# One layer of convolution and attention: the first image begins with the middle taps, its weights are built in small steps, weight loads move to ScalarE's queue, scaled output sums are put off

## The chip, the cores and the metric

The kernel runs on one core of one Trainium2 chip. Its time is the device time of one execution in microseconds (us). All arithmetic is float32. The engines are named TensorE (PE in profiles; its weight loads are PEld), VectorE (DVE), ScalarE (ACT), GpSimd (POOL) and SyncE (SP, which here only issues DMAs).

## The reference

Four images x of 128 channels and 64 by 64 pixels go through two layers. The change touches only the first. After a group norm it sums three padded convolutions (7x7, 5x5 and 3x3, 128 to 128 channels) with a non-local attention block and its residual, applies a relu and adds x:

```
g = _gn(x)                                  # 32 groups of 4 channels
y = conv2d(g, w7, b7, 3) + conv2d(g, w5, b5, 2) + conv2d(g, w3, b3, 1)
f = einsum('bcn,bcm->bnm', theta, phi) / sqrt(64)     # 4096 x 4096 scores for each image
out = einsum('bcm,bnm->bcn', g_x, softmax(f))         # then a 1x1 convolution, plus g
x = x + relu(y + nonlocal(g))               # what the kernel computes of layer 0
```

The second layer takes the pixels as 4096 tokens: a layer norm, a state-space block in both directions, another layer norm, a batch norm over all tokens, and a recurrence over the tokens. Its code is the same before and after.

## The kernel before

**Stages.** `conv_attention` does layer 0 for all images (it fills the first 1736 us of the profiled span), `mamba` and `recurrence` do layer 1. The running image values live in one SBUF tensor `t` of four images; the outputs of layer 0 overwrite the image they belong to.

**Convolution.** The three kernels are summed into one 7x7 kernel. Its middle row stays as it is (`wc`). The other rows are applied as a polynomial product: the input rows are combined into forms and multiplied by combined weights at the points 0, +U, -U, +V, -V and infinity. This gives eight pieces of work, numbered `m`: 0 and 5 (the two end points, which also take the middle row on other rows), 1 and 2 (plus and minus U), 3 and 4 (plus and minus V), 6 and 7 (the middle row alone, with the input rows as they are). A piece with m below 6 has three products n = 0, 1, 2, each with a weight tile of its own: 18 tiles of 576 KB, `wd`, in HBM. `convolve` loads them one by one into `wt` (L377, a pool of two buffers, on SyncE's queue), multiplies (L364), and combines the results `eo` on ScalarE (L383), VectorE (L385 to L391) and GpSimd (L397 to L419). Pieces 1 and 3 only keep their result (`mid`). Piece 2 adds and subtracts it and writes four output phases: one on GpSimd, and three scaled ones on ScalarE, put off with `later`. Piece 4 adds to these four: one on GpSimd (L411) and three scaled ones at once on VectorE, in two halves each (L414).

**Attention.** A step handles 512 queries: eight iterations of `scores` (L437, then the exponential on ScalarE, L439, into `ex`, four buffers) and `values` (L448), while VectorE sums the exponentials into `es` (L452, L454). Then comes one piece of convolution, with `divide` (the reciprocal, L460) and `collect` (L468 to L470, which adds finished attention outputs to `t`) between its products. So an image is eight steps, and layer 0 is 32 steps. I number them 0 to 31. `forms` builds the inputs of the step's convolution on ScalarE and GpSimd while the attention runs.

**Order of pieces.** `ORDER = (1, 2, 0, 6, 7, 5, 3, 4)` for images 0 to 2, and `LAST = (1, 2, 3, 4, 6, 7, 5, 0)` for image 3.

**Order on the engines.** TensorE and ScalarE are under `manual_schedule`: their instructions stand as the program writes them. VectorE, GpSimd and SyncE are ordered by the scheduler when the program is built, and every engine then takes its own list strictly in order. `later(f)` appends to the list `late`, from which each iteration of the attention takes one entry: it decides where the call stands in the program.

**Weights.** The generator `weights` loads w7, w5 and w3 into the space of image 1 in `t`, sums them (L512, L513), forms sums and differences along x (`thirds`, L520 to L522, over seven rows at once), copies the middle row to `wc` (L526), and then forms the 18 tiles (`pair`, L540 to L542, and `store`, L531, L533). Everything up to and including pieces 1 and 2 is asked for before step 0, the ends before step 1, pieces 3 and 4 before step 2. Image 1 is loaded over this space afterwards (L1641); `statistics` (L238) reads it.

**Finish.** `finish(b)` queues eight parts for the image before: a load of x into `xr` (L475, SyncE, two buffers), a relu on ScalarE (L477), an add on GpSimd (L478).

Of the kernel before, what the change touches and what calls it, by code (L numbers as in the profile page):

```python
# [10 lines left out]
F32 = mybir.dt.float32  # L11
AF = mybir.ActivationFunctionType
ALU = mybir.AluOpType
# [3 lines left out]
P = 128  # L17
NC = 512
# [135 lines left out]
def conv_attention(nc, tc, k, a, t, B, H, W, flags, load, mem, loads):  # L154
# [21 lines left out]
    KB, PC = H // 4, W // 2  # L176
# [10 lines left out]
    with ExitStack() as ctx:  # L187
# [176 lines left out]
                    nc.tensor.matmul(pm[:, e, :], wt, src, start=(i == 0), stop=(i == len(terms) - 1))  # L364
            return pm

        def convolve(b, m, f):

            image = t[:, b * T : (b + 1) * T].rearrange("p (k g j c x) -> p g j x k c", g=2, j=4, c=PC, x=2)
            base = None  # L370
            for n in range(3):
                if f[n] is None:
                    continue
                wt = wc
                if m < 6:
                    wt = fm.tile([P, 9, P], F32, tag="wt", name="wt")
                    nc.sync.dma_start(wt, wd[3 * m + n])  # L377
                fn = [v + (u,) for v, u in zip(f[n], (wt, wc))]
# [3 lines left out]
                by = BY.get(m, 1.0)  # L382
                nc.scalar.mul(eo[:, 1, :], pm[:, 1, :], by / 2)  # L383
                for e, op in enumerate((ALU.add, ALU.subtract)):
                    nc.vector.scalar_tensor_tensor(eo[:, e, :], pm[:, 0, :], by / 2, eo[:, 1, :], ALU.mult, op)  # L385
# [12 lines left out]
                out = lambda j: image[:, n - 1, j]  # L398
                in_ = lambda v: v.rearrange("p x (k c) -> p x k c", c=PC)
                if keep:  # L400
                    mid[n] = eo
                elif m == 2:
                    nc.gpsimd.tensor_tensor(out(0), in_(mid[n]), in_(eo), ALU.add)
                    nc.gpsimd.tensor_tensor(mid[n], mid[n], eo, ALU.subtract)
                    for j, v, by in ((2, out(0), UU), (1, in_(mid[n]), U), (3, in_(mid[n]), U * UU)):
                        later(nc.scalar.mul, out(j), v, by)
                elif m == 4:
                    u = wk.tile([P, 2, KB // 2 * PC], F32, tag="u", name="u", bufs=2)
                    nc.gpsimd.tensor_tensor(u, mid[n], eo, ALU.add)
                    nc.gpsimd.tensor_tensor(mid[n], mid[n], eo, ALU.subtract)  # L410
                    nc.gpsimd.tensor_tensor(out(0), out(0), in_(u), ALU.add)  # L411
                    for j, v, by in ((2, u, VV), (1, mid[n], V), (3, mid[n], V * VV)):
                        for x in range(2):
                            nc.vector.scalar_tensor_tensor(  # L414
                                out(j)[:, x], in_(v)[:, x], by, out(j)[:, x], ALU.mult, ALU.add
                            )
                else:
                    j = {0: 0, 5: 3, 6: 1, 7: 2}[m]
                    nc.gpsimd.tensor_tensor(out(j), out(j), in_(eo), ALU.add)  # L419
                yield  # L420

        def queries(n):
# [33 lines left out]
        def divide(n, acc, es):  # L456
            den = ps_c.tile([P, NC], F32, tag="c", name="den")
            nc.tensor.matmul(den, k.ones, es[:, 0, :], start=True, stop=True)
            att = wk.tile([P, NC], F32, tag="att", name="att", bufs=3)
# [23 lines left out]
        def later(f, *args):  # L483

            late.append(lambda: f(*args))
# [17 lines left out]
        def weights():  # L503

            w = t[:, T : T + 63 * P].rearrange("p (y x o) -> p y x o", y=7, x=9)
            free = t[:, T + 63 * P : T + 90 * P].rearrange("p (n o) -> p n o", o=P)
            w5 = free[:, 0:25].rearrange("p (y x) o -> p y x o", y=5)
            w3 = wc.rearrange("p (y x) o -> p y x o", y=3)
            nc.sync.dma_start(w[:, :, 0:7, :], a["w7t"].rearrange("i (y x) o -> i y x o", y=7))
            nc.sync.dma_start(w5, a["w5t"].rearrange("i (y x) o -> i y x o", y=5))  # L510
            nc.sync.dma_start(w3, a["w3t"].rearrange("i (y x) o -> i y x o", y=3))
            nc.vector.tensor_tensor(w[:, 1:6, 1:6, :], w[:, 1:6, 1:6, :], w5, ALU.add)  # L512
            nc.gpsimd.tensor_tensor(w[:, 2:5, 2:5, :], w[:, 2:5, 2:5, :], w3, ALU.add)  # L513

            nc.vector.scalar_tensor_tensor(w[:, 3, 3, :], k.ident, 2.0, w[:, 3, 3, :], ALU.mult, ALU.add)

            def thirds(g, new):

                ac = free[:, 0 : new.shape[1], :]
                nc.vector.tensor_tensor(ac, g[0], g[2], ALU.add)  # L520
                nc.gpsimd.tensor_tensor(new, ac, g[1], ALU.subtract)
                nc.vector.tensor_tensor(g[1], ac, g[1], ALU.add)  # L522
# [12 lines left out]
            def pair(m, at):  # L535

                spare = [fm.tile([P, 9, P], F32, tag="wt", name="ws") for _ in range(2)]
                made = []
                for g, e, f in zip(lots, (slot[0], slot[2]), (slot[1], spare[0])):
                    nc.vector.scalar_tensor_tensor(e, g[:, 2], at * at, g[:, 0], ALU.mult, ALU.add)  # L540
                    nc.vector.scalar_tensor_tensor(f, g[:, 1], at, e, ALU.mult, ALU.add)
                    nc.vector.scalar_tensor_tensor(e, g[:, 1], -at, e, ALU.mult, ALU.add)  # L542
                    made.append((f, e))
                store(m, slot[3], *(v[0] for v in made))
                store(m + 1, spare[1], *(v[1] for v in made))

            pair(1, U)
            yield
            for m, i in ((0, 0), (5, 2)):
                store(m, slot[i], *(g[:, i] for g in lots))  # L550
            yield
            pair(3, V)
            yield

        phi = big.tile([P, NT // 2, P], F32, name="phi")
        gT = big.tile([P, NT, IC], F32, name="gT")
        gn, mid, atts, xl, late = {}, {}, {}, [], []
# [20 lines left out]
        for n in range(N):  # L578
            b, q = divmod(n, NQ)
            more = b + 1 < B and q == NQ - 1  # L580
            if n in (1, 2):
                next(making)
            if 3 <= n < B + 2:
                load(n - 2)
            m = (ORDER if b + 1 < B else LAST)[q]
            f = []
            making_forms = forms(m, f)
            next(making_forms, None)
            if b + 1 < B and q == NQ - 3:
# [15 lines left out]
            for i, _ in enumerate(convolve(b, m, f)):  # L605
# [1093 lines left out]
```

## Time and profile before

| | |
|---|---|
| three runs | 3225.29, 3225.89 and 3230.95 us, median 3225.89 |
| the profiled execution | 3225.68 us, span 3224.0 us |
| layer 0 in the span | 0 to 1736 us (the attention steps from 35.57 us) |
| TensorE matmul, busy | 2959.4 us (92%) |
| VectorE, ScalarE, GpSimd, busy | 2279.3, 1805.0 and 1805.3 us |
| bytes by DMA | 224.15 MB, mean 70 GB/s |

The shares are averages over stages that differ. The chain of waits on the page, followed back from the last instruction, reaches 1765 us and no further, so it tells nothing of layer 0, where the change lies. There the boundaries of the 32 steps are read from TensorE's timeline: a step begins at the first score matmul after a convolution. A step's length is then compared with that of a step of the same piece without a stall.

### The profile page before, as it was taken

Reading aid. Unit: us, or ns where it says so; the run is one execution under the profiler, and the core shown is the slowest. Engines: PE = TensorE matmul, PEld = TensorE weight load, DVE = VectorE, ACT = ScalarE, POOL = GpSimd, SP = SyncE. Lnnn points to the kernel's source line nnn. Section 1 sums busy time; section 2 is a strip of 40 time slices with the busy share of each in tenths; the row PEclk is TensorE's granted clock in tenths of the full one; section 3 lists DMA queues with packets and bytes.
Section 4 is the critical chain, followed back from the end, with each engine's and each line's share of the span. In section 5 each row is a group of like instructions: output and inputs, shape, how many; then the busy total and the mean of one; then the engine's idle time right before and its main releaser. Section 6 shows DMA issues by size and latency. Waiting matters only on the chain. (4 is left out here: it accounts for less than half of the span.)

```text
span 3224.0 us, 42883 instructions
## 1 busy us (share of the span) xinstructions
PE 2959.4 (92%) x15511; PEld 1467.2 (46%) x15511; DVE 2279.3 (71%) x3458; ACT 1805.0 (56%) x3078; POOL 1805.3 (56%) x1369
## 2 busy tenths in 40 slices
PE   5889999899988999899998899999999999999986
PEld 1444444445443544344354354444444444454545
DVE  6676677766876677767666676767667767777667
ACT  3224434333435334343432787887788778888756
POOL 5461757825758446677165266556655664565654
PEclk8999999999999999999998899999999999999988
DMA  4230001100011001021002334333433343334332
GB/s 170 81 138 8 23 31 37 56 15 23 23 38 55 23 8 37 22 64 37 8 23 86 87 93 118 96 93 93 114 91 97 88 113 92 102 93 99 90 113 106
DMA packets 108394, 224.15 MB, mean 70 GB/s; under 512 B 25679, under 2 KB 29391, under 8 KB 106765
## 3 DMA queue, kind: packets, MB, share of 16 engines
q1 hardware_dynamic: 106956, 220.01, 23.7%
q8 instruction: 125, 2.05, 0.3%
q10 hardware_dynamic: 1216, 1.31, 0.1%
q14 instruction: 97, 0.79, 0.1%
HBM read 200.83 MB, written 20.44 MB: 69 GB/s over the span
## 5 line engine op out<-in xcount | busy, mean ns | idle before, releaser
L454 DVE TENSOR_TENSOR es<-es,ex 128x1024 f32<-128x1024 f32 x448 | 722.5, 1613 | 117.9 <-ACT ex L439 79.5
L439 ACT ACTIVATE ex<-pf 128x1024 f32<-128x1024 f32 x512 | 500.8, 1023 | 490.6 <-PE pf L437 381.4
L437 PE MATMUL pf<-theta,phi 64*128 64x512 f32 x2048 | 523.2, 629 | 58.2 <-ACT ex L439 56.8
L448 PE MATMUL acc<-ex,gT 128*64 128x512 f32 x2048 | 495.1, 609 | 13.5 <-ACT ex L439 13.5
L1147 POOL TENSOR_TENSOR ct<-ct,Cst 128x512 f32<-128x512 f32 x128 | 169.3, 1323 | 404.8 <-DMA ct<-csmem 363.5
L437 PEld LDWEIGHTS pf<-theta,phi 64*128 64x128 f32 x2048 | 175.0, 189 | 382.7 <-ACT ex L439 242.6
L364 PE MATMUL pm<-yf,wt 128*128 128x256 f32 x1152 | 293.6, 388 | 23.1 <-DMA wt<-wd 23.1
L1113 ACT ACTIVATE lt<-lt,cs 128x128 f32<-128x128 f32 x1024 | 312.1, 390 | 0.0
L383 ACT ACTIVATE eo<-pm 128x256 f32<-128x256 f32 x88 | 33.8, 384 | 481.7 <-PE pm L364 481.7
L448 PEld LDWEIGHTS acc<-ex,gT 128*64 128x64 f32 x2048 | 127.9, 137 | 356.6 <-issue 330.2
L364 PEld LDWEIGHTS pm<-yf,wt 128*128 128x128 f32 x1152 | 218.1, 193 | 98.7 <-issue 54.5
L335 POOL TENSOR_TENSOR yf<-yd 128x272 f32<-128x272 f32 x192 | 243.5, 1300 | 0.0
L1048 PE MATMUL pb<-tl,wbc_fwd 128*64 128x512 f32 x512 | 236.8, 606 | 2.4 <-DVE xT L1080 2.4
L1048 PE MATMUL pb<-tl,wbc_bwd 128*64 128x512 f32 x512 | 237.4, 606 | 0.0
L397 POOL TENSOR_TENSOR eo<-eo 128x512 f32<-128x512 f32 x48 | 62.9, 1310 | 288.3 <-DVE eo L391 220.3
L419 POOL TENSOR_TENSOR t<-t,eo 128x512 f32<-128x512 f32 x32 | 44.0, 1375 | 301.2 <-DVE eo L389 300.0
L1212 POOL TENSOR_TENSOR yT<-yT,zT 128x512 f32<-128x512 f32 x127 | 167.3, 1327 | 34.7 <-DVE yT L1199 30.5
L1146 DVE TENSOR_TENSOR lt<-lt,gm 128x1024 f32<-128x1024 f32 x128 | 182.5, 1425 | 1.9
L385 DVE SCALAR_TENSOR_TENSOR eo<-pm,eo 128x256 f32<-128x256 f32 x176 | 73.5, 418 | 117.4 <-ACT eo L383 115.0
L1080 DVE SCALAR_TENSOR_TENSOR xT<-px,taps_bwd,xT 128x512 f32<-128x512 f32 x192 | 143.7, 749 | 8.2 <-ACT xT L1074 3.3
L335 POOL TENSOR_TENSOR yf<-yx 128x272 f32<-128x272 f32 x96 | 148.0, 1570 | 1.9
L1179 PE MATMUL y<-lt,xdt 128*64 128x128 f32 x2048 | 141.7, 281 | 7.7 <-PE ptr L1122 3.4
(295 smaller groups left out, 5777.2 us busy)
## 6 DMA issues: line engine op xcount, KB each, us to landing
lt<-csmem SPq DMA_DIRECT2D x128, 512.0 KB, 5.7
wt<-wd SPq DMA_DIRECT2D x72, 576.0 KB, 3.7
ct<-csmem SPq DMA_DIRECT2D x256, 128.0 KB, 5.3
rs<-m SPq DMA_DIRECT2D x31, 512.0 KB, 4.1
t<-in_x SPq DMA_DIRECT2D x4, 2048.0 KB
rows<-after SPq DMA_DIRECT2D x32, 256.0 KB, 4.4
out<-t SPq DMA_DIRECT2D x4, 2048.0 KB, 14.4
wd<-t SPq DMA_DIRECT2D x14, 576.0 KB, 3.3
```

Source lines behind the costliest of these rows:

```text
L335: nc.gpsimd.tensor_tensor(f[:, kx], at(x), at(y), op)
L364: nc.tensor.matmul(pm[:, e, :], wt, src, start=(i == 0), stop=(i == len(terms) - 1))
L437: nc.tensor.matmul(pf[:, e, :], phi[HALF[e], m, :], th[HALF[e]], start=True, stop=True)
L439: nc.scalar.activation(ex, pf, AF.Exp, scale=scale)
L448: nc.tensor.matmul(acc[HALF[e]], gT[:, 2 * m + e, :], ex[:, e, :], start=(m == 0), stop=(m == NT // 2 - 1))
L454: nc.vector.tensor_tensor(es, es, ex, ALU.add)
L1048: nc.tensor.matmul(out, w[i]["bc"][:, tap, bass.ts(c, DS)], src, start=(tap == 0), stop=(tap == KC - 1),)
L1080: nc.vector.scalar_tensor_tensor(at(n), px, taps[:, PAD - n : KC - n], at(n), ALU.mult, ALU.add)
L1113: nc.scalar.activation(v, v, AF.Relu, scale=-1.0, bias=m["b"]["cs"][:, d, m["i"], h : h + 1])
L1146: nc.vector.tensor_tensor(lt, lt, gm.unsqueeze(2).to_broadcast([P, ND, NHEAD, P]), ALU.mult)
L1147: nc.gpsimd.tensor_tensor(m["ct"], m["ct"], Cs[:, cols].unsqueeze(1).to_broadcast([P, NHEAD, P]), ALU.mult)
L1212: eng.tensor_tensor(v, v, gr["z"][d][:, :, half(d, j // 2)], ALU.mult)
```

## The change

1. Image 0 takes its pieces in the order `FIRST = (6, 7, 1, 2, 0, 5, 3, 4)`. Since outputs may now first be written by any piece, `put` keeps a set `begun` and copies (or scales) the first time and adds afterwards. In image 0, attention outputs are collected in the fifth step instead of the third (`att` gets four buffers instead of three).
2. `weights` builds the middle row first and the rest in 24 small pieces, one taken in each iteration of the attention.
3. The loads of weight tiles go to ScalarE's queue: tiles 0 and 1 in the next to last iteration of the attention, tile 2 behind the scaling of the second product.
4. Piece 4 puts off its three scaled sums with `later`, as piece 2 does. Where an output phase has begun, a scaled sum is two VectorE instructions.

```diff
+        def fetch(m, n):
+            wt = fm.tile([P, 9, P], F32, tag="wt", name="wt")
+            nc.scalar.dma_start(wt, wd[3 * m + n])
+            return wt
+            def put(n, j, v, by=1.0):
+                out = image[:, n - 1, j]
+                if (b, n, j) not in begun:
+                    begun.add((b, n, j))
+                    if by == 1.0:
+                        nc.gpsimd.tensor_copy(out, v)
+                    else:
+                        nc.scalar.mul(out, v, by)
+                elif by == 1.0:
+                    nc.gpsimd.tensor_tensor(out, out, v, ALU.add)
+                else:
+                    for x in range(2):
+                        nc.vector.scalar_tensor_tensor(out[:, x], v[:, x], by, out[:, x], ALU.mult, ALU.add)
...
-                    nc.sync.dma_start(wt, wd[3 * m + n])
...
                 nc.scalar.mul(eo[:, 1, :], pm[:, 1, :], by / 2)
+                if wts and n == 1:
+                    wts.append(fetch(m, 2))
...
-                    for j, v, by in ((2, out(0), UU), (1, in_(mid[n]), U), (3, in_(mid[n]), U * UU)):
-                        later(nc.scalar.mul, out(j), v, by)
+                    for j, v, c in ((2, out, UU), (1, in_(mid[n]), U), (3, in_(mid[n]), U * UU)):
+                        later(put, n, j, v, c)
...
-                    for j, v, by in ((2, u, VV), (1, mid[n], V), (3, mid[n], V * VV)):
-                        for x in range(2):
-                            nc.vector.scalar_tensor_tensor(
-                                out(j)[:, x], in_(v)[:, x], by, out(j)[:, x], ALU.mult, ALU.add
-                            )
+                    put(n, 0, in_(u))
+                    for j, v, c in ((2, u, VV), (1, mid[n], V), (3, mid[n], V * VV)):
+                        later(put, n, j, in_(v), c)
...
-            nc.vector.tensor_tensor(w[:, 1:6, 1:6, :], w[:, 1:6, 1:6, :], w5, ALU.add)
-            nc.gpsimd.tensor_tensor(w[:, 2:5, 2:5, :], w[:, 2:5, 2:5, :], w3, ALU.add)
+            sums(3, 4)
             nc.vector.scalar_tensor_tensor(w[:, 3, 3, :], k.ident, 2.0, w[:, 3, 3, :], ALU.mult, ALU.add)
             for s in SLOT:
-                thirds([w[:, :, s[i], :] for i in (0, 1, 3)], w[:, :, s[2], :])
+                thirds(3, 4, s)
+            sums(1, 3)
+            yield
+            sums(4, 6)
             nc.gpsimd.tensor_copy(wc, w[:, 3])
+            yield
+            for s in SLOT:
+                for y in (0, 4):
+                    thirds(y, y + 3, s)
+                    yield
...
+            yield from pair(1, U, (slot[0:2], slot[2:4]), spare)
             for m, i in ((0, 0), (5, 2)):
                 store(m, slot[i], *(g[:, i] for g in lots))
+                yield
+            yield from pair(3, V, [(g[:, 2], g[:, 0]) for g in lots], (slot[1], slot[3]))
...
+        FIRST = (6, 7, 1, 2, 0, 5, 3, 4)
...
-            if n in (1, 2):
-                next(making)
...
                 next(making_forms, None)
+                next(making, None)
+                if m < 6 and i == NB - 2:
+                    wts = [fetch(m, 0), fetch(m, 1)]
                 if late:
                     late.pop(0)()
...
-                    if q != 1:
+                    if q not in ((1, 2, 3) if b == 0 else (1,)):
                         for o in sorted(atts):
                             collect(o, atts.pop(o))
```

`sums(y0, y1)` adds w5 (VectorE) and w3 (GpSimd) to the rows y0 to y1 of w7. `pair` yields after each instruction and after each stored piece.

More of the change, by code (lines that the diff above doesn't have):

```diff
@@ L365, in products, with convolve @@
             return pm
-        def convolve(b, m, f):
-            image = t[:, b * T : (b + 1) * T].rearrange("p (k g j c x) -> p g j x k c", g=2, j=4, c=PC, x=2)
+        def fetch(m, n):
+            wt = fm.tile([P, 9, P], F32, tag="wt", name="wt")
+            nc.scalar.dma_start(wt, wd[3 * m + n])
+            return wt
+        def convolve(b, m, f, wts):
+            image = t[:, b * T : (b + 1) * T].rearrange("p (k g j c x) -> p g j x k c", g=2, j=4, c=PC, x=2)
+            in_ = lambda v: v.rearrange("p x (k c) -> p x k c", c=PC)
+            def put(n, j, v, by=1.0):
[11 more added lines that the diff above has]
+                        nc.vector.scalar_tensor_tensor(out[:, x], v[:, x], by, out[:, x], ALU.mult, ALU.add)
+            by = BY.get(m, 1.0)
             base = None
@@ L373, in convolve @@
                     continue
[L374 to L378, printed above, removed]
+                fn = [v + (u,) for v, u in zip(f[n], (wts[n], wc) if wts else (wc,))]
                 pm = products(fn, (1, 2))
@@ L381, in convolve @@
                 eo = wk.tile([P, 2, KB // 2 * PC], F32, tag=f"mid{n}" if keep else "eo", name="eo", bufs=1 if keep else 4)
-                by = BY.get(m, 1.0)
                 nc.scalar.mul(eo[:, 1, :], pm[:, 1, :], by / 2)
+                if wts and n == 1:
+                    wts.append(fetch(m, 2))
                 for e, op in enumerate((ALU.add, ALU.subtract)):
@@ L397, in convolve @@
                     nc.gpsimd.tensor_tensor(eo, eo, base, ALU.add)
-                out = lambda j: image[:, n - 1, j]
-                in_ = lambda v: v.rearrange("p x (k c) -> p x k c", c=PC)
                 if keep:
@@ L402, in convolve @@
                 elif m == 2:
-                    nc.gpsimd.tensor_tensor(out(0), in_(mid[n]), in_(eo), ALU.add)
+                    begun.add((b, n, 0))
+                    out = image[:, n - 1, 0]
+                    nc.gpsimd.tensor_tensor(out, in_(mid[n]), in_(eo), ALU.add)
                     nc.gpsimd.tensor_tensor(mid[n], mid[n], eo, ALU.subtract)
-                    for j, v, by in ((2, out(0), UU), (1, in_(mid[n]), U), (3, in_(mid[n]), U * UU)):
-                        later(nc.scalar.mul, out(j), v, by)
+                    for j, v, c in ((2, out, UU), (1, in_(mid[n]), U), (3, in_(mid[n]), U * UU)):
+                        later(put, n, j, v, c)
                 elif m == 4:
@@ L410, in convolve @@
                     nc.gpsimd.tensor_tensor(mid[n], mid[n], eo, ALU.subtract)
-                    nc.gpsimd.tensor_tensor(out(0), out(0), in_(u), ALU.add)
-                    for j, v, by in ((2, u, VV), (1, mid[n], V), (3, mid[n], V * VV)):
-                        for x in range(2):
-                            nc.vector.scalar_tensor_tensor(
-                                out(j)[:, x], in_(v)[:, x], by, out(j)[:, x], ALU.mult, ALU.add
-                            )
-                else:
-                    j = {0: 0, 5: 3, 6: 1, 7: 2}[m]
-                    nc.gpsimd.tensor_tensor(out(j), out(j), in_(eo), ALU.add)
+                    put(n, 0, in_(u))
+                    for j, v, c in ((2, u, VV), (1, mid[n], V), (3, mid[n], V * VV)):
+                        later(put, n, j, in_(v), c)
+                else:
+                    put(n, {0: 0, 5: 3, 6: 1, 7: 2}[m], in_(eo))
                 yield
@@ L458, in divide @@
             nc.tensor.matmul(den, k.ones, es[:, 0, :], start=True, stop=True)
-            att = wk.tile([P, NC], F32, tag="att", name="att", bufs=3)
+            att = wk.tile([P, NC], F32, tag="att", name="att", bufs=4)
             nc.vector.reciprocal(att, den)
@@ L511, in weights, with sums, thirds @@
             nc.sync.dma_start(w3, a["w3t"].rearrange("i (y x) o -> i y x o", y=3))
-            nc.vector.tensor_tensor(w[:, 1:6, 1:6, :], w[:, 1:6, 1:6, :], w5, ALU.add)
-            nc.gpsimd.tensor_tensor(w[:, 2:5, 2:5, :], w[:, 2:5, 2:5, :], w3, ALU.add)
-            nc.vector.scalar_tensor_tensor(w[:, 3, 3, :], k.ident, 2.0, w[:, 3, 3, :], ALU.mult, ALU.add)
[L517 to L522, printed above, removed]
+            def sums(y0, y1):
+                nc.vector.tensor_tensor(
+                    w[:, y0:y1, 1:6, :], w[:, y0:y1, 1:6, :], w5[:, y0 - 1 : y1 - 1], ALU.add
+                )
+                z0, z1 = max(y0, 2), min(y1, 5)
+                nc.gpsimd.tensor_tensor(
+                    w[:, z0:z1, 2:5, :], w[:, z0:z1, 2:5, :], w3[:, z0 - 2 : z1 - 2], ALU.add
+                )
+            def thirds(y0, y1, s):
+                v, new = [w[:, y0:y1, s[i], :] for i in (0, 1, 3)], w[:, y0:y1, s[2], :]
+                ac = free[:, 25 : 25 + y1 - y0, :] if y1 - y0 == 1 else free[:, 0 : y1 - y0, :]
+                nc.vector.tensor_tensor(ac, v[0], v[2], ALU.add)
+                nc.gpsimd.tensor_tensor(new, ac, v[1], ALU.subtract)
+                nc.vector.tensor_tensor(v[1], ac, v[1], ALU.add)
+            sums(3, 4)
+            nc.vector.scalar_tensor_tensor(w[:, 3, 3, :], k.ident, 2.0, w[:, 3, 3, :], ALU.mult, ALU.add)
             for s in SLOT:
-                thirds([w[:, :, s[i], :] for i in (0, 1, 3)], w[:, :, s[2], :])
+                thirds(3, 4, s)
+            sums(1, 3)
+            yield
+            sums(4, 6)
             nc.gpsimd.tensor_copy(wc, w[:, 3])
+            yield
[3 more added lines that the diff above has]
+                    yield
             slot = [free[:, bass.ts(i, 9), :] for i in range(3)] + [w[:, 3]]
@@ L533, in store, with pair @@
                     nc.sync.dma_start(wd[3 * m + n], v)
[L535 to L539, printed above, removed]
+            def pair(m, at, places, boths):
+                for g, (e, f) in zip(lots, places):
                     nc.vector.scalar_tensor_tensor(e, g[:, 2], at * at, g[:, 0], ALU.mult, ALU.add)
+                    yield
                     nc.vector.scalar_tensor_tensor(f, g[:, 1], at, e, ALU.mult, ALU.add)
+                    yield
                     nc.vector.scalar_tensor_tensor(e, g[:, 1], -at, e, ALU.mult, ALU.add)
[L543 to L548, printed above, removed]
+                    yield
+                for i in range(2):
+                    store(m + i, boths[i], *(v[1 - i] for v in places))
+                    yield
+            spare = [fm.tile([P, 9, P], F32, tag="wt", name="ws") for _ in range(2)]
+            yield from pair(1, U, (slot[0:2], slot[2:4]), spare)
             for m, i in ((0, 0), (5, 2)):
                 store(m, slot[i], *(g[:, i] for g in lots))
-            yield
-            pair(3, V)
-            yield
+                yield
+            yield from pair(3, V, [(g[:, 2], g[:, 0]) for g in lots], (slot[1], slot[3]))
         phi = big.tile([P, NT // 2, P], F32, name="phi")
         gT = big.tile([P, NT, IC], F32, name="gT")
-        gn, mid, atts, xl, late = {}, {}, {}, [], []
+        gn, mid, atts, xl, late, begun = {}, {}, {}, [], [], set()
         NB = NT // 4
         N = B * NQ
+        FIRST = (6, 7, 1, 2, 0, 5, 3, 4)
         ORDER = (1, 2, 0, 6, 7, 5, 3, 4)
@@ L580, in conv_attention @@
             more = b + 1 < B and q == NQ - 1
-            if n in (1, 2):
-                next(making)
             if 3 <= n < B + 2:
                 load(n - 2)
-            m = (ORDER if b + 1 < B else LAST)[q]
-            f = []
+            m = (FIRST if b == 0 else ORDER if b + 1 < B else LAST)[q]
+            f, wts = [], None
             making_forms = forms(m, f)
@@ L603, in conv_attention @@
             nc.vector.tensor_tensor(es[:, 0, :], es[:, 0, :], es[:, 1, :], ALU.add)
-            for i, _ in enumerate(convolve(b, m, f)):
+            for i, _ in enumerate(convolve(b, m, f, wts)):
                 if i == 0:
-                    if q != 1:
+                    if q not in ((1, 2, 3) if b == 0 else (1,)):
                         for o in sorted(atts):
```

## The prediction

> **What bounds the kernel now.** The chain of waits begins at 1765 us, so for layer 0 I read TensorE's timeline, cut it into the 32 steps, and asked for busy time and clock in single steps. The columns are the stretch, its length, busy time (and count) of PE, PEld, DVE, ACT and POOL, then clock, DMA share and GB/s.
>
> ```profile
> 35.57:119.52 83.95, 51.22 (x192) 21.84 (x192) 59.16 (x44) 21.77 (x25) 46.18 (x25) 0.82 0.37 134
> 119.52:165.12 45.60, 45.33 (x193) 21.39 (x192) 37.25 (x30) 18.32 (x21) 29.63 (x18) 1.00 0.11 39
> 165.12:241.92 76.80, 61.61 (x238) 30.62 (x237) 54.07 (x60) 23.16 (x28) 49.80 (x44) 0.91 0.36 137
> 489.92:545.06 55.14, 49.28 (x196) 22.37 (x195) 44.98 (x39) 20.60 (x23) 36.05 (x22) 0.94 0.10 33
> 545.06:602.38 57.32, 48.40 (x197) 23.50 (x196) 37.37 (x38) 23.20 (x29) 42.45 (x28) 0.91 0.21 68
> ```
>
> Step 1 (second row) is a step without stall: TensorE is busy for 45.33 of 45.60 us at clock 1.00. Undisturbed, TensorE bounds layer 0, and a step with a piece of 1 to 4 lasts 45.6 us. Steps 0, 2, 8 and 9 (the other rows) are far longer, and their clock is below 1. The difference is what can be won. Steps 16 and 24 repeat step 8 (56.08 and 54.13 us), 17 and 25 repeat step 9 (57.06 and 53.01 us), and step 28, after the last image's piece 4, lasts 51.02 against 42.17 us. The waits of TensorE in layer 0 (total, times, longest) name two causes:
>
> ```profile
> PE pf L437 <- ACT ex L439: 56.8, 40, 17.3
> PE pm L364 <- DMA wt<-wd: 23.1, 3, 9.5
> PE den L458 <- DVE eo L385: 10.6, 4, 7.5
> ```
>
> The timeline shows what stands behind them.
>
> ```profile
> 64.52 16.88 DVE L454 TENSOR_TENSOR es<-es,ex 128x1024 f32<-128x1024 f32 x8
> 66.90 2.08 PE L437 MATMUL pf<-theta,phi 64*128 64x512 f32 x4 [17.26 <-ACT ex L439]
> ...
> 187.78 0.69 DVE L238 BATCH_NORM_STATS2 st<-t 128x6 f32<-128x512 f32 x1 [6.20 <-DMA t<-in_x]
> ...
> 496.17 7.11 DVE L414 SCALAR_TENSOR_TENSOR t<-eo,t 128x256 f32<-128x256 f32 x4
> 505.59 3.78 PE L437 MATMUL pf<-theta,phi 64*128 64x512 f32 x8 [5.51 <-ACT ex L439]
> ...
> 576.60 14.32 SPq L475 DMA_DIRECT2D xr<-in_x  x8
> 590.97 68.06 SPq L377 DMA_DIRECT2D wt<-wd  x6
> 595.44 5.22 PE L364 MATMUL pm<-yf,wt 128*128 128x256 f32 x12 [8.65 <-DMA wt<-wd]
> ```
>
> At 66.90 TensorE has waited 17.26 us: an exponential needs a buffer that the sums es free, and these waited until 64.52 behind weight making. In step 2 the statistics stand in VectorE's list between the sums and wait for an image. In step 8 the scaled sums of piece 4 (four in 7.11 us, beside GpSimd) hold up the sums. In step 9 SyncE must first issue the finish loads xr, each waiting for a buffer, and the weight tile comes late.
>
> **Weight loads, won.** Without stall steps 9, 17 and 25 would last 45.60 plus 0.45 us (four transposes) = 46.05. They lose 11.27 + 11.01 + 6.96 = 29.2 us, the slow clock after the wait included. From ScalarE's queue, tiles 0 and 1 are asked for well ahead, and no load of xr is in front. All of the 29.2 goes.
>
> The Trainium skill ("DMA: Bandwidth & Descriptors", section "Issuing engines are not separate DMA queues") says that issuing from several engines saves only the sequencer's issue time. A weight load's issue takes 0.32 us in this trace; an estimate by that rule alone would be three such issues, 1 us instead of 29.2. The trace disagrees here: the tile was not slow but not asked for, the issuing engine waiting in order at 576.60 to 590.9 for GpSimd.
>
> **Weight loads, lost.** Tile 2 now stands behind ScalarE's scaling of the second product. In step 0 of before that is at 111.72 to 112.10 us, and TensorE wants tile 2 at 115.05. SyncE asked at about 109.8 and was in time. From issue to landing takes 3.3 us at least, 3.7 median, 6.1 at most: issued at 112.0 it lands at 115.3 to 118.1, and the stall is 0.25 to 3.05 us. I take 0.9, the median and a short start. It holds for pieces 1 to 4 except where keys of the next image are made in between (steps 7, 15, 23): 13 steps. Pieces 0 and 5 have twelve matmuls there (5 us) and hide it. In steps 9, 17 and 25 the load also waits in the built program for an xr load: 1.5 us. Sum 10 x 0.9 + 3 x 1.5 = 13.5 us. What is queued behind the load on ScalarE, the theta activation, has 8 us of slack.
>
> **Deferred sums of piece 4: nothing.** They are VectorE instructions, and VectorE's list is the scheduler's. In the changed program as built all twelve still stand ahead of the first sum es of the next step, in all images. The 8.7 + 9.6 + 7.7 + 8.9 = 34.9 us lost in steps 8, 16, 24 and 28 (against 46.46 and 42.17 us) stay.
>
> **New in step 4.** In image 0 pieces 6 and 7 write before piece 2, so four of its six scaled outputs become VectorE pairs instead of ScalarE scalings: eight instructions behind GpSimd's chain. By the rows of step 8 (wait 2.7, pair 1.85, two beside GpSimd 3.6 us) the first es begins 11.5 us into step 4; in step 8 it began at 13.3 and cost 8.7 us, normal is 3.2. I take 5.5 us lost, bounds 2 and 9. Four collects at once cost no more matmuls than before, one by one.
>
> **Weights in small steps.** All the work still lies in step 0: the built list has all twelve multiply-adds (L540 to L542 before) there, now alternating with the sums. GpSimd's list puts 16 forms for pieces 6 and 7 before the weight sums: 0.61 us each (8 in 4.9 us), from 22.6 to 32.4 us; at the mean of this form over layer 0, 0.86, to 36.3. That is hidden, since the first es comes at 38.7 anyway. Then VectorE and GpSimd take turns: a copy 2.33, two small and four subtractions of 384 elements (0.4 and 0.9, from 2.08 for 896), and four times two VectorE pieces of 0.45: 10.3 us, to 50.3. Then 12 multiply-adds x 1.36 (row 92.71) and 14 sums x 1.22 and 0.69: 34.1 us, if GpSimd is quiet. But six GpSimd adds of 1152 elements lie beside it. The eight sums at 64.52 took 2.11 us each beside GpSimd, 0.9 more; over 21.6 us (six at 3.6) that is 9 us, and a further 3 for the ends' add, which waits for stored tiles: 12 us. Bounds 0 and 21.6. So es ends at 96.4 (84.4 to 106). In step 3 the step ends 11.6 us after es: 108.0. Step 0 then lasts 72.4 instead of 42.17, an excess of 30.3 against 83.95 - 45.60 = 38.35 before. Gain 8 us (-2 to 20).
>
> The Trainium skill ("SBUF — State Buffer", section "SBUF: two separate sides") has VectorE with two SBUF inputs and GpSimd take a shared port as an exclusive lock for a whole instruction. By that an estimate would be six blockings of up to 3.6 us, 21.6 instead of 12, and a gain of -2 us. This trace's longest such sum beside GpSimd is 3.53 us, as the rule has it, but the mean 2.11 is what adds up.
>
> **Statistics.** They move from step 2 to step 1. The last tile is stored after GpSimd's last add, about 97.5; 4 us to land, then image 1 in 8 us (as at the start, 0.82 to 8.84): 110, in a step that begins at 108. The first es is 3 us late, and 24 statistics of 0.62 us among ten sums push the tenth to 8 us late; 1 us of slack. Excess 7 (3 to 15) against 76.80 - 57.26 = 19.5 in step 2 before. Gain 12.5 us.
>
> **Sum**, against the profiled 3225.7 us (span 3224.0 and 1.7 around it; 0.2 below the median): - 29.2 + 13.5 + 5.5 - 8 - 12.5 = - 30.7, **3195 us**.
>
> **Rivals.**
> *The first image wins nothing.* VectorE is the bound while weights are made, and it is not relieved of work. For it: 46 us of GpSimd work in step 0 beside 59 of VectorE. At the upper bound of contention the 20.5 us fall away: 3215 us (3205 to 3223).
> *Tile 2 makes it slower.* Place: the third product of 13 steps; price: what the load is later than TensorE. All gains are used up at (30.7 + 13.5) / 13 = 3.4 us per step, a landing of 6.5 us. For it: landings of 6.1 occur, and ScalarE waits in order, for xr loads too. Against: the median 3.7. At 5 us a step: 3246 us.
> *The deferral works after all*, the sums es running first: another 34.9 us, 3160. Against it stands the built list.
>
> **How the numbers follow.** Forecast 0.58 (3182 to 3210), nothing in the first image 0.18, tile 2 0.17, deferral 0.07. About 0.2% (6.5 us) is what a measurement can tell. Faster: 0.58 + 0.07 and 0.10 of the second case, 0.75; its other 0.08 is the same; tile 2 is slower, 0.17. The range 3172 to 3232 leaves out deferral and all of tile 2 but its mildest quarter (up to 3.9 us per step, 13 x 0.5 = 6.5 above the break-even), 0.07 + 0.13 = 0.20.
>
> **What would show it.** Right: steps 9, 17 and 25 near 47.5 us without the 23.1 us of waits for weight tiles; a new wait of TensorE for wt of about 1 us, some 13 times; steps 8, 16, 24 and 28 as long as before; step 0 near 72 and step 1 near 49 us with statistics waiting for an image. Wrong: tile waits above 3 us, a step 8 below 48 us, a step 0 below 60 or above 82 us.

## The result and the profile after

The changed kernel takes 3202.42 us (median; 3201.2 to 3204.34) against 3226.3 us for the kernel before, timed on the same chip: a ratio of 0.9924, 95% interval 0.9907 to 0.9941. It is faster by 0.8%. The prediction was 3195 us, in a range of 3172 to 3232. The profiled executions took 3203.28 and 3225.68 us, so 22.4 us are to be accounted for where the prediction had 30.7.

I cut the 32 steps from TensorE's timeline again and asked for the busy time in the same kinds of step (columns as before: stretch, length, PE, PEld, DVE, ACT, POOL with counts, clock, DMA share, GB/s). These rows are steps 0, 1, 4, 8 and 9 of the changed kernel:

```profile
33.38:106.25 72.87, 50.77 (x173) 20.38 (x173) 57.11 (x51) 18.10 (x21) 37.66 (x21) 0.81 0.46 171
106.25:151.91 45.66, 42.12 (x174) 17.27 (x173) 40.71 (x52) 17.40 (x19) 1.30 (x2) 1.00 0.26 110
247.54:313.29 65.75, 59.90 (x241) 30.88 (x241) 45.87 (x42) 20.67 (x24) 41.82 (x30) 0.95 0.08 28
480.52:535.07 54.55, 48.21 (x195) 22.01 (x194) 45.01 (x39) 20.60 (x23) 36.07 (x22) 0.97 0.09 33
535.07:583.10 48.03, 46.06 (x197) 21.81 (x196) 36.79 (x38) 23.20 (x29) 39.02 (x26) 1.00 0.24 77
```

Step 9 (last row) has lost its stall: 57.32 us before, 48.03 now, and the clock is 1.00 instead of 0.91. Step 8 is what it was (55.14, now 54.55). Step 0 is shorter by 11 us, of which 4.3 are its piece: a middle tap lasts 42.17 us without a stall, less 0.86 us for a collect, which step 0 does not make (0.86 is 46.46 - 45.60, a step of pieces 1 to 4 with a collect and one without), against 45.60 for piece 1. VectorE is still busy for 57 of its 73 us.

The waits of TensorE in layer 0 (total, times, longest):

```profile
PE pf L453 <- ACT ex L455: 47.5, 42, 6.6
PE pm L364 <- DMA wt<-wd: 20.5, 28, 3.5
PE den L474 <- DVE es L639: 11.6, 6, 7.7
```

Two things stand out. The longest wait for an exponential fell from 17.3 to 6.6 us. The waits for weight tiles fell only from 23.1 to 20.5 us, but they changed their form: three long ones became 28 short ones. The timeline shows where they are.

```profile
63.80 11.98 DVE L470 TENSOR_TENSOR es<-es,ex 128x1024 f32<-128x1024 f32 x4
61.55 9.58 POOL L564 TENSOR_TENSOR ws<-t 128x1152 f32<-128x1152 f32 x2 [11.68 <-DVE t L573]
109.38 4.25 DVE L238 BATCH_NORM_STATS2 st<-t 128x6 f32<-128x512 f32 x7 [2.34 <-DMA t<-in_x]
179.23 0.36 ACTq L369 DMA_DIRECT2D wt<-wd  x1
183.86 1.97 PE L364 MATMUL pm<-yf,wt 128*128 128x256 f32 x8 [1.15 <-DMA wt<-wd]
486.77 7.11 DVE L390 SCALAR_TENSOR_TENSOR t<-eo,t 128x256 f32<-128x256 f32 x4
566.62 10.24 SPq L491 DMA_DIRECT2D xr<-in_x  x6
573.54 0.33 ACTq L369 DMA_DIRECT2D wt<-wd  x1
578.55 1.75 PE L364 MATMUL pm<-yf,wt 128*128 128x256 f32 x7 [1.14 <-DMA wt<-wd]
```

In step 9 SyncE's queue still stands in its xr loads from 566.62 on, but the weight tile no longer stands behind them: ScalarE issues it at 573.54, and TensorE is 1.14 us early for it. That is tile 2. At 183.86, however, TensorE waits for tile 0, which was issued at 179.23, 3.5 us before TensorE wanted it. In step 0 four sums beside GpSimd's adds of weights take 11.98 us from the first to the last. Of their own they lasted (least, median and longest, in ns):

```profile
L470 DVE TENSOR_TENSOR es<-es,ex x4: 1214/3472/3508, 63.8 to 72.3; 128x1024 f32<-128x1024 f32 x4
```

So one took 1.21 us and three about 3.5. The statistics now stand at the beginning of step 1. The scaled sums of piece 4 still stand ahead of the sums es in step 8 and take the same 7.11 us as before.

### The profile page after: what moved, and what is told of

It is laid out like the page before. It is cut to its first block, busy times and chain, and to the rows that moved or that the text cites. A ratio compares the mean times of both kernels' runs of the same rounds, so it can differ in the third digit from the quotient of the medians.

```text
span 3201.6 us, 42877 instructions
## 1 busy us (share of the span) xinstructions
PE 2957.4 (92%) x15511; PEld 1463.9 (46%) x15511; DVE 2288.2 (71%) x3476; ACT 1803.1 (56%) x3074; POOL 1824.4 (57%) x1375
## 5 line engine op out<-in xcount | busy, mean ns | idle before, releaser
L470 DVE TENSOR_TENSOR es<-es,ex 128x1024 f32<-128x1024 f32 x448 | 730.5, 1630 | 108.2 <-ACT ex L455 69.5
L453 PE MATMUL pf<-theta,phi 64*128 64x512 f32 x2048 | 524.1, 630 | 49.0 <-ACT ex L455 47.5
L364 PE MATMUL pm<-yf,wt 128*128 128x256 f32 x1152 | 286.6, 381 | 21.5 <-DMA wt<-wd 20.5
L335 POOL TENSOR_TENSOR yf<-yd 128x272 f32<-128x272 f32 x192 | 253.0, 1349 | 0.0
```

Source lines behind the costliest of these rows:

```text
L335: nc.gpsimd.tensor_tensor(f[:, kx], at(x), at(y), op)
L453: nc.tensor.matmul(pf[:, e, :], phi[HALF[e], m, :], th[HALF[e]], start=True, stop=True)
L470: nc.vector.tensor_tensor(es, es, ex, ALU.add)
```

## Experiments

All runs are compared with the kernel before on the same chip, whose median lay between 3223.61 and 3226.3 us on these chips, so ratios compare better than times; the ratio of the changed kernel itself is 0.9924 (0.9907 to 0.9941). Layer 1, whose code is the same in all of these kernels, lasted between 1486.5 and 1496.2 us in their profiles, so of a single profile I use the steps of layer 0 and not its span.

**1. The loads back on SyncE's queue.**

```diff
-            nc.scalar.dma_start(wt, wd[3 * m + n])
+            nc.sync.dma_start(wt, wd[3 * m + n])     # and fetched in convolve, product by product
```

> The changed kernel, with the weight loads back on SyncE's queue, asked for where each product begins in the program, as before the change. Theory (the queue is worth what steps 9, 17 and 25 show): these three steps get back their 9.3 + 8.9 + 6.2 = 24.4 us, and the waits for late tiles in the other steps, 20.5 - 4.9 = 15.6 us in the profile after, go away: +8.8 us, 3211 us (3206 to 3218). Rival (the weight waits of before were an effect of the order of pieces and of where weights are stored, not of the queue): it stays at 3202 us, without a wait of more than 2 us for wt in steps 9, 17 and 25.

Measured: 3214.39 us, ratio 0.9970 (0.996 to 0.998). Steps 9, 17 and 25 lasted 56.79, 57.07 and 53.08 us, 24.0 us more than in the changed kernel, and the three long waits were back:

```profile
PE pm L364 <- DMA wt<-wd: 23.0, 3, 9.4
```

The other steps from step 1 on became 11.7 us shorter, without their late tiles (15.6 us of waits were expected to go). So the queue is worth 0.46% net (0.9970 - 0.9924), by the mechanism that was read from the profile before.

**2. The queue alone.** The kernel before, with only the loads moved to ScalarE's queue at the places of the changed kernel.

> The kernel before, with only the weight loads moved to ScalarE's queue, at the places of the changed kernel. Theory (the two parts add up): as much as the changed kernel loses with its loads back on SyncE's queue, 12 to 15 us: 3226 - 13 = 3213 us (3207 to 3219), steps 9, 17 and 25 near 48 us, and the first image's steps as before the change. Rival (in step 0 the loads stand in ScalarE's list ahead of the scalings and wait for tiles that are still being made): steps 0 to 2 grow, and more than 3220 us.

Measured: 3216.49 us, ratio 0.9971 (0.9961 to 0.9981). Steps 9, 17 and 25: 47.93, 47.83 and 47.44 us. The first image kept its long steps 0 and 2 (84.56 and 73.98 us). So the queue alone brings 0.3% (8.6 us, where 12 to 15 were expected), and so does the rest of the change without it (experiment 1). The product of both ratios is 0.9941, the changed kernel has 0.9924; the difference is within the intervals.

**3. Tiles 0 and 1 two iterations earlier.**

```diff
-                if m < 6 and i == NB - 2:
+                if m < 6 and i == NB - 4:
```

> The changed kernel, with tiles 0 and 1 asked for two attention iterations earlier (about 7.6 us). Theory (the wait is the time from issue to landing, 3.7 us or more, since tile 0 is issued only some 4.5 us before its first product): the waits of the first product, 14.3 of the 20.5 us, go, the 6.1 us of tile 2 stay: 3188 us (3184 to 3192). Rival (the tiles come late because transfers are slow or wait for a buffer): they land as late as now, 3202 us. Second rival (the issue holds up the exponentials on ScalarE): more than 3205 us.

Measured: 3195.99 us, ratio 0.9916 (0.9903 to 0.993). The waits for tiles fell from 20.5 to 6.7 us, as the theory has it, but layer 0 from the end of step 0 on got shorter by 4.6 us only, 3.5 of them in step 31 (59.03 to 55.51 us). So the time misses the theory's range. Step 10 shows why. First the waits in the changed kernel, then in this one, in the same step (58.74 and 58.73 us long):

```profile
PE pm L364 <- DMA wt<-wd: 1.1, 1, 1.1
PE den L474 <- DVE eo L405: 0.6, 1, 0.6
```

```profile
PE den L474 <- DVE eo L405: 1.7, 1, 1.7
```

The 1.1 us moved over, unchanged, to the matmul den, which needs the whole sum of VectorE: the late tile had hidden a late sum.

**4. Tile 2 with them, into a third buffer.**

```diff
-                    wts = [fetch(m, 0), fetch(m, 1)]                      # i == NB - 2
+                    wts = [fetch(m, 0), fetch(m, 1), fetch(m, 2)]         # i == NB - 4, tag wt with bufs=3
```

> Tiles 0 and 1 asked for two iterations earlier, as before, and tile 2 with them, into a third buffer. Theory (tile 2 waits for the scaling of the second product and lands up to 1.7 us late): the remaining 6.7 us of waits for wt go, but as with tile 0 a part was covered by VectorE anyway: 3 to 6 us under the run with tiles 0 and 1 early. Rival (all of it was covered): the same time as that run, with waits of TensorE for es or eo in place of those for wt.

Measured: 3189.36 us, ratio 0.989 (0.9876 to 0.9904). No wait for a tile is left in layer 0, and steps 9, 17 and 25 last 46.04, 45.60 and 45.60 us. From the end of step 0 on layer 0 is 12.2 us shorter than in the changed kernel, for 20.5 us of waits removed. Most of the missing 8 us is found in the waits for den, which were 11.6 and 1.5 us in the changed kernel and are now:

```profile
PE den L472 <- DVE es L637: 14.1, 6, 7.1
PE den L472 <- DVE eo L403: 4.8, 2, 2.4
```

These matmuls need VectorE's whole sum, so 5.8 us had been covered by VectorE. The rest is not accounted for, and the 12.2 us come from one profile of each kernel: step 5 alone is 2.0 us shorter here, for a reason that no run here shows. Against experiment 3 the time is 6.6 us lower, a little more than the 3 to 6 expected.

**5. Weights in three large steps as before, the new order of pieces kept.**

> The changed kernel, with the weight making as it was before: over seven rows at once, in three large steps asked for ahead of steps 0, 1 and 2; the new order of pieces and the rest stay. Theory (the gain of step 0 comes from sums es alternating with small pieces of weight making): step 0 is as long as before the change but for the middle piece that needs no tile, 83.95 - 3.4 = 80.5 us instead of 72.9, so 3210 us; and pieces 3 and 4 are again made around step 2, where the statistics wait: up to 3222 us. Rival (the order of pieces alone does it): 3202 us, step 0 near 73 us.

Measured: 3204.96 us, ratio 0.9936 (0.9923 to 0.995); steps 0 to 2 last 73.92, 43.64 and 48.67 us, together 166.2 against 167.1. The rival is right: the small steps bring nothing that these runs can tell from noise. TensorE's longest wait for an exponential is 14.0 us again instead of 6.6, but the last sum of step 0 ends at 96.4 us, 1.7 later than in the changed kernel. A longer stall in the middle of the step costs next to nothing if VectorE ends at nearly the same time.

**6. VectorE in the order of the program.** VectorE joins TensorE and ScalarE under `manual_schedule`.

> The changed kernel, with VectorE's instructions of layer 0 in the order of the program, as TensorE's and ScalarE's are. Theory (the scheduler's list undoes the small steps and the deferral): the multiply-adds lie one per two sums es over steps 0 to 2, so step 0 falls from 72.9 to some 46 to 50 us and the statistics disturb nothing (steps 1, 4 and 5 lose some 10 us of their excess); the scaled sums of piece 4 stand behind the first sums, so steps 8, 16, 24 and 28 lose most of their 33 us of excess: 3202 - 25 - 10 - 28 = 3139 us (3125 to 3165). Rival (in the order of the program VectorE waits for TensorE's results where the scheduler had put other work): every step grows, more than 3202 us.

Measured: 3291.08 us, ratio 1.0219 (1.0202 to 1.0235). The rival is right, in places. Step 0 fell to 50.27 us, but step 2 rose to 70.67: steps 0 to 2 take 168.2 us. The making of weights only moved. Steps 7, 15 and 23, where keys are made between the products, grew by 17 us each, because VectorE's part of the keys stands behind other work and TensorE waits for it:

```profile
PE pp L265 <- DVE xn L260: 37.6, 13, 6.4
```

Steps 5, 13 and 21, which make the next image's statistics between the products, grew by 26.5 us together; there TensorE waits for the statistics:

```profile
PE pm L242 <- DVE mv L240: 13.2, 3, 5.0
```

The deferral of piece 4 now works: the first sum stands ahead of the scaled sums, and then two of these lie between every two sums. Step 28 is 6.7 us shorter (43.22 us), but steps 8, 16 and 24 are 2.6 to 2.8 us longer (57.26, 57.69 and 57.60 us): in step 8 VectorE's last sum ends 42.7 us into the step, 40.1 in the changed kernel. So the scheduler's order is not the only reason that the deferral does nothing there.

**7. Without the scaled sums of piece 4.**

> The changed kernel without the scaled sums of piece 4 (output phases 1 to 3 lack this part). Theory (these sums on VectorE are all that makes steps 8, 16, 24 and 28 long): they fall from 54.55, 55.05, 54.81 and 49.87 us to 46.5 and 42.2: 3202 - 33 = 3169 us. Rival (the sums es are slow beside GpSimd at the start of these steps whatever stands ahead of them, as the run with VectorE in the order of the program hints, where steps 8, 16 and 24 lasted 57 us with the scaled sums put off): they stay above 50 us, 3185 us or more.

Measured: 3185.95 us, ratio 0.9872 (0.9858 to 0.9887). Step 28 lost its whole excess (42.16 us); steps 8, 16 and 24 lost only a third to a half of theirs: 50.62, 50.49 and 52.25 us. The timeline of step 8 shows what remains:

```profile
486.36 18.70 DVE L468 TENSOR_TENSOR es<-es,ex 128x1024 f32<-128x1024 f32 x8 [1.66 <-ACT ex L453]
487.05 3.47 POOL L296 TENSOR_TENSOR yb<-yb,xp 128x1190 f32<-128x1190 f32 x1
490.48 3.49 POOL L296 TENSOR_TENSOR yx<-yx,xp 128x1190 f32<-128x1190 f32 x1
```

The eight sums take 18.70 us from the first to the last: 1.48 to 3.54 us each beside GpSimd's work on the forms, where one alone takes 1.21. In step 28 the piece, a middle tap, needs no adds of 1190 elements. So in steps 8, 16 and 24 the scaled sums are one cause of the loss; that GpSimd's adds are the other is read from the timeline and not shown by a run, and weight tiles have a part in what remains (1.1 us of waits in step 8, 2.4 in step 24).

**8. Scaling on ScalarE, add on GpSimd.**

```diff
-                    for x in range(2):
-                        nc.vector.scalar_tensor_tensor(out[:, x], v[:, x], by, out[:, x], ALU.mult, ALU.add)
+                    s = wk.tile([P, 2, KB // 2 * PC], F32, tag="s4", name="s4", bufs=2)
+                    nc.scalar.mul(in_(s), v, by)
+                    nc.gpsimd.tensor_tensor(out, out, in_(s), ALU.add)
```

> The changed kernel, with each scaled sum made as a scaling on ScalarE (in the order of the program, so put off in fact) and an add on GpSimd, instead of two instructions on VectorE. Theory (VectorE is what is short at the start of steps 4, 8, 16, 24 and 28): it is rid of twelve instructions, 11 to 22 us, in each; ScalarE is busy for 20.6 of 54.6 us in step 8 and takes six scalings of about 0.7 us, GpSimd for 36.1 and takes six adds of about 1.45 us: 3202 - 28 = 3174 us (3165 to 3190). Rival (GpSimd becomes the bound: the forms for the step's convolution come 9 us later, or its adds slow the sums as much): 3200 us or more, with TensorE waiting for yf.

Measured: 3229.83 us, ratio 1.0011 (1.0001 to 1.002); steps 8, 16 and 24 lasted 63.29, 63.22 and 63.92 us. Step 28 gained (44.33 us). Neither theory named what happened in step 8. ScalarE waits there:

```profile
ACT s L390 <- POOL t L391: 18.8, 3, 13.2
PE pf L454 <- ACT ex L456: 14.0, 3, 11.8
```

A scaling needs one of the two buffers s, which GpSimd frees only after its adds for the forms. The exponentials are queued behind the scaling on ScalarE, and TensorE waits for them (second line).

**9. Weight adds on VectorE.**

```diff
-                nc.gpsimd.tensor_tensor(both, *own, ALU.add)
+                nc.vector.tensor_tensor(both, *own, ALU.add)
```

> The changed kernel, with the six adds of 1152 elements that finish the weight tiles on VectorE instead of GpSimd. Theory (of the prediction: they cost VectorE about 12 us by standing beside its sums): in the profile after, four sums beside them took 11.98 us instead of 4.9, the last add 2.98 instead of 1.02, and VectorE waited 2.5 us for one of them, 11.5 us; on VectorE they cost 6 x 1.3 = 8 us: step 0 falls by 3.5 us to 69.4 us, 3199 us. Rival (a lock for a whole instruction, 21.6 us): step 0 near 60 us, 3189 us. Second rival (VectorE's own work is the bound, and GpSimd beside it costs little): step 0 grows by 5 us or more.

Measured: 3199.85 us, ratio 0.9921 (0.9908 to 0.9933); step 0 fell from 72.87 to 66.48 us, and step 1 grew by 1.5. Here is the same stretch of step 0:

```profile
63.62 1.22 DVE L470 TENSOR_TENSOR es<-es,ex 128x1024 f32<-128x1024 f32 x1
64.76 2.62 DVE L564 TENSOR_TENSOR ws<-t 128x1152 f32<-128x1152 f32 x2
67.29 1.22 DVE L470 TENSOR_TENSOR es<-es,ex 128x1024 f32<-128x1024 f32 x1
```

Every sum takes 1.22 us now. VectorE took on six adds (2.62 + 4 x 1.36 = 8.1 us). Five of them stand ahead of its last sum of the step and take 6.3 us of its time, and still this sum ends at 88.49 us instead of 94.69. So GpSimd's adds had cost it some 12.4 us up to there: three sums of about 3.5 us instead of 1.22, a last sum (half as long) of 2.98 instead of 0.70, and 2.5 us of waiting for an add. The gain is one of step 0: with step 1 and the rest, layer 0 is only 1.4 us shorter, and the time is not clear of that of the changed kernel.

**10. Five buffers ex instead of four.**

> The changed kernel, with five buffers ex instead of four. Theory (at the start of steps 4, 8, 16, 24 and 28 the sums are late by a few, and TensorE stops because four exponentials wait for them; VectorE is busy for 45 of the 54.6 us of step 8 and could catch up): each of the five steps loses one sum's time, 2 us or more, and more where the clock stays at 1.00: 3202 - 12 = 3190 us. Rival (VectorE is late until the end of the step): the wait moves to the matmul den, which needs the whole sum: 3202 us.

Measured: 3203.31 us, ratio 0.9932 (0.992 to 0.9945): no gain over the changed kernel, as the rival has it. In layer 0 part of the wait moved:

```profile
PE pf L453 <- ACT ex L455: 36.6, 36, 5.6
PE den L474 <- DVE es L639: 19.4, 7, 12.1
```

The 12.1 us are in step 0, where this wait was 7.7 us; the step lasts 72.87 us as before. In steps 4, 8, 16, 24 and 28 the waits for exponentials fell by 1.0 to 1.2 us each without moving to den, and the five steps became 1.9 us shorter in all, not the 10 or more that the theory has.

**11. Scaled sums at once.** Piece 4 asks for them as before the change, without `later`.

> The changed kernel, with the scaled sums of piece 4 asked for at once, as before the change, instead of with later. Theory (of the prediction: VectorE's list is the scheduler's, and in the built program the two differ only by a few neighbouring instructions): steps 8, 16, 24 and 28 stay within 1.5 us of 54.55, 55.05, 54.81 and 49.87 us, and the time within 4 us of 3202. Rival (the deferral is worth something): these steps grow by 2 us or more each, 3210 us or more.

Measured: 3208.71 us, ratio 0.9944 (0.9931 to 0.9958). Steps 8, 16, 24 and 28 lasted 55.72, 56.52, 55.18 and 50.45 us, 3.6 us more in all and each within the 1.5 us of the theory. The time is not within its 4 us and comes near the rival's; but in the profiles layer 0 ends only 2.5 us later than in the changed kernel, and the rest of the difference is in layer 1, whose code is the same. By the steps the deferral as written is worth 0 to 4 us.

**12. What helped, together.** Experiments 4 and 9, and in the last image the scaled sums as scalings in place on ScalarE and adds on GpSimd.

> All three tiles early, the third in a buffer of its own; the six weight adds on VectorE; and in the last image the scaled sums of piece 4 as a scaling in place on ScalarE and an add on GpSimd. Theory (they add up): 3189 - 2.6 from the adds - 5.5 in step 28 (49.9 to 44.3 us, as in the run with all scaled sums on ScalarE and GpSimd) = 3181 us (3176 to 3187). Rival (the adds of GpSimd in step 28 come beside the sums, as in steps 8, 16 and 24 of that run): step 28 stays near 50 us, 3187 us.

Measured: 3186.40 us, ratio 0.9875 (0.986 to 0.9889), the lowest median of a version that computes the whole reference, though its interval overlaps that of experiment 4. Step 0 lasts 66.53 us, step 28 47.83 instead of 49.87: between theory and rival. The sums in step 28 took 1.2 to 2.3 us each, where all took 1.2 in the changed kernel, with GpSimd's adds now beside them.

## Why the prediction was right, and where its terms were off

Against the profiled execution of before, with steps of the same piece without a stall as the measure:

| term | predicted | measured |
|---|---|---|
| steps 9, 17, 25: loads won, tile 2 late | -29.2 + 4.5 = -24.7 | -24.4 |
| step 0, making weights | -8 | -6.8 |
| statistics (steps 1 and 5) | -12.5 | -12.3 |
| step 4, new scaled sums | +5.5 | +6.8 |
| steps 2, 3, 6 and 7 (late tiles) | +2.7 | +5.1 |
| other steps of images 1 to 3 | +6.3 | +7.9 |
| beginning of step 0 | 0 | -2.2 |
| layer 1 | 0 | +3.5 |
| sum | -30.7 | -22.4 |

The measure of the first image counts the collects, 0.86 us each on TensorE: steps 0 and 1 make none and step 4 four, where steps of the same pieces elsewhere make one, one and two. The prediction took 42.17 us for step 0, with a collect.

**Loads won: right.** The steps were forecast at 47.5 us and lasted 48.03, 48.12 and 46.84. There was a little more to win than 29.2 us: steps 17 and 25 last 45.60 us without a stall (experiment 4), not 46.05. Experiments 1 and 2 move just this term, in both directions. The Trainium skill ("DMA: Bandwidth & Descriptors", section "Issuing engines are not separate DMA queues") led to 1 us; the measurement decides against it here, since what the other engine saved was not the issue but the place in a line in which each entry waits for a buffer.

**Loads lost: the size was near, the working failed.** The step that failed is "tiles 0 and 1 are asked for well ahead". They stand two iterations before the end in the program, but on ScalarE behind the last exponentials, so they are issued some 3.5 us before their use and need at least 3.4 us (median 3.8, longest 5.9). Of the 20.5 us of waits 14.3 are theirs, 17 times, all for tile 0. Tile 2 was forecast at 13.5 us and waits 11 times, 6.1 us in all, with 1.7 at most. A second omission helped: some 8 of the 20.5 us cost nothing, most of them because they lay beside a late sum of VectorE (experiments 3 and 4). What was left, 12.2 us, is near the 13.5 by luck. In steps 2, 3, 6 and 7 only 2.5 of the 5.1 us went with the late tiles in experiment 4; the rest is in step 2, where a late sum lay under them (a wait for den of 2.0 us there). The worst single wait, 3.48 us in step 31, had its loads issued beside that of the last image. It is above the 3 us that the prediction named as a sign of being wrong.

**Step 0: right in its length (72.4 forecast, 72.87), with errors in its working.** GpSimd's adds were put at 12 us and cost some 12.4 (experiment 9), but by luck: the mean of 2.11 us that went into the 12 was taken over eight sums of 1.21 to 3.53 us with a median of 1.49, of which only two took 3.4 us or more. The Trainium skill's exclusive lock ("SBUF — State Buffer", section "SBUF: two separate sides") led to an estimate of 21.6. The trace agrees with the lock for each sum that met such an add (about 3.5 us, where an add alone took 2.81), but not with the sum of six: of the six adds, which lasted 24.9 us in all, three held up a long sum, one the last short one, and one stood beside a VectorE that waited for it. And the small steps have no share in the gain (experiment 5). What of the new order brings it, that the forms of the first pieces are simpler or that their weights need no tile, was not separated.

**Statistics: right.** They stand in step 1 and wait 2.34 us for the image. Step 1 is 4.3 us longer than without a stall, and step 5 up to 2.9 (it varied from 57.1 to 59.2 us between the kernels with this order and VectorE under the scheduler), against 19.5 in step 2 before. The forecast had 7, all in step 1.

**Step 4: the right mechanism, mis-sized.** The sum es begins 12.5 us into the step (forecast 11.5) and it loses 6.8 us instead of 5.5, inside the bounds of 2 and 9. The second pair took 5.58 us beside GpSimd, not the 3.6 assumed.

**Deferral: right that it does nothing, half right why.** The built order was one reason. The other, by the timeline, is that VectorE and GpSimd slow each other at the start of steps 8, 16 and 24, whatever the order (experiments 6 and 7). The rival in which it works was given 34.9 us; in experiment 6, where it does, step 28 won 6.7 us and the other three steps won nothing.

**The rest of the miss** is layer 1, +3.5 us, which lies within the spread of its 14 profiles, and the start of step 0. The earlier start is no gain of its own: in experiments 1 and 4 step 0 began at 35.2 us instead of 33.4, lasted 70.1 and ended at 105.3, 1 us earlier than in the changed kernel. Its end follows VectorE's last sum.

## What to carry to other kernels

A load should be asked for on an engine whose list does not stand behind other waits; then count from the instruction it stands behind, not from its line in the program, to its use, and compare that with the time to landing. Before counting a wait as a gain, ask what is late next: here some 8 of 20.5 us of tile waits cost nothing, most of them over a late sum, and with a fifth buffer the wait in step 0 only moved. In step 0, which VectorE bounds, cutting its work into smaller pieces changed nothing; taking GpSimd's work from beside it did, even when VectorE had to do it.

## What the runs showed of the hardware

- VectorE and GpSimd slow each other: a sum of 1024 elements takes 1.22 us alone, about 3.5 when it meets a GpSimd add of 1152 elements, and an add of 1152 takes 2.81 us while VectorE waits and up to 5.97 beside its work. Six such adds cost VectorE some 12.4 us, more than it needs to do them itself (8.1 us).
- A 576 KB tile lands 3.4 to 5.9 us after its issue from ScalarE's queue (median 3.8; 4.8 in experiment 4, where three are asked for together); an issue takes 0.33 us.
- Layer 1 with the same code took 1486.5 to 1496.2 us in 14 profiles, so a difference of some us in one profile's span shows nothing by itself.
